# Softmax maxima spread over the partitions: transposes on TensorE, or a round trip through HBM and a ScalarE copy into PSUM

## The chip, the core and the metric

The kernel runs on one core of a Trainium2 chip (trn2). Time is device microseconds of one execution; 3 runs of the kernel before are given. TensorE is PE (its weight loads are PEld), VectorE is DVE, ScalarE is ACT, GpSimd is POOL, and SyncE is SP, which issues nearly all DMAs from one queue, in order.

## What is computed

Everything is float32. Eight images of 512 channels and 32x32 positions go through two layers. The first is a group norm, then a block of 1x1 and 3x3 convolutions with two attention stages, then a residual sum. The second is a group norm, a masked 1x1 convolution and a residual sum. The change touches the attention:

```python
def bot_attention(x, qkv_w, rw, rh):
    b, c, h, w = x.shape
    hw = h * w                                        # 1024 positions
    qkv = conv2d(x, qkv_w, 0).reshape(b, 3, HEADS, HD, hw)   # 4 heads of 64
    q, k, v = (qkv[:, 0], qkv[:, 1], qkv[:, 2])
    r = (rw + rh).reshape(1, HEADS, HD, hw)
    logits = jnp.einsum('bhdi,bhdj->bhij', q, k + r) * HD ** (-0.5)
    a = jax.nn.softmax(logits, axis=-1)
    out = jnp.einsum('bhij,bhdj->bhdi', a, v)
    return out.reshape(b, c, h, w)
```

## The kernel before

**Units.** Attention is cut into 64 units (`class Unit`): image `n`, block `i` of two, head pair `hp`, and `half` of the 1024 queries. A unit's name is `n_i_hp_half`, so `2_1_1_1` is the last unit of image 2 in block 1. Logits lie transposed, keys on the partitions and 512 queries along the free dimension, two heads side by side. A unit has eight key tiles `t` (KT = 8) of 128 keys.

**The steps of a unit.** `logits(t)` multiplies (L494, tile `lg`, a PSUM bank for each head), copies both banks into the SBUF tile `st` (ScalarE, L500), and takes a running maximum over the key tiles into `mx` (VectorE, L505). `mx` then holds, for each query, a maximum for each of the 128 partitions. `top()` transposes `mx` in blocks of 128 queries on TensorE (L513, PSUM tile `mt`), so that queries lie on partitions, and reduces along the free dimension with a change of sign (VectorE, L514). The result is the small tile `nm`, 128x2x4, with the negated maximum of every query. The softmax needs that number on all 128 partitions, again along the free dimension. `spread()` does this: eight transposes, each of a column of `nm` stretched to 128x128 by a step of zero (L521), into the two-bank PSUM tile `mb`. `soften(t)` adds `mb` to `st` (VectorE, L525) and exponentiates in place (ScalarE, L526); GpSimd sums the exponentials of all tiles (L531). `values(t)` multiplies `st` by `v` into `po` (TensorE, L537). `finish()` sums over partitions with a matrix of ones (L549, `den`), copies it (L551), and `divide()` takes the reciprocal on VectorE (L556) and scales `po`.

**Who sets the order.** The main loop (L980 to L1036) goes through 16 slots of an image and a block, four units each. It writes out the steps of a unit, the logits of the next unit between them, and other work of the same or other images as filler: `advance(share)` takes pieces from `slot_filler` (3x3 convolutions of the next slot, projections, and the 1x1 convolutions of the `Background` list) until a share of the slot's filler is done. A slot has 4 x 10 such steps. `Clock` holds operations that are due some time later by an estimate of passed time. The framework's scheduler then orders each engine's instructions by its own estimate of when each could start; `in_turn` and `add_manual_dep` with `IN_ORDER` fix the order of some without a wait. Each engine executes its own queue strictly in that order, so an instruction that waits holds up all behind it.

**Memory.** PSUM's eight banks are `ps_m` (2 banks, `mb`), `ps_o` (1 bank, `po`) and `ps_f` (5 banks in rotation, for all else). In SBUF, `st` tiles come from 10 buffers, the weights from 4, `k` and `v` from 3 each, and the temporaries of the 3x3 convolution's input transform (`wt`: `a`, `b`, `a2`, `b2`) from 3. The small parameters (`bn_sb`, `s_sb`, `rw_sb`, `rh_sb`, and `tri`) have tiles of their own. The helper `load` (L77) issues a DMA on SP.

The step before the first exponentials in the main loop is this:

```python
u.top()
clock.tick(0.9)
advance((base + 1) / steps)
u.spread()
clock.tick(0.9)
advance((base + 2) / steps)
```

Of the kernel before, what the change touches and what calls it, by code (L numbers as in the profile page):

```python
# [15 lines left out]
F32 = mybir.dt.float32  # L16
# [6 lines left out]
P = 128  # L23
# [16 lines left out]
def conv_preact_kernel(ctx: ExitStack, tc: tile.TileContext, x, cv1, cv2, mcv1, qkv, mcv2, bn, rw, rh, conv, s_in, t_in, out):  # L40
# [18 lines left out]
    tp = pool("tp", 3)  # L59
    wt = pool("wt", 3)  # L60
    ps_m = pool("ps_m", 1, space=PSUM)
# [23 lines left out]

    bn_sb = const.tile([P, 4, BN_ALL], F32, name="bn_sb")
    s_sb = const.tile([P, 2, CT, NG], F32, name="s_sb")
    rw_sb = const.tile([P, NBLK, IT, F], F32, name="rw_sb")
    rh_sb = const.tile([P, NBLK, IT, F], F32, name="rh_sb")

# [4 lines left out]

    y_dram = [[dram.tile([P, IT, HW], F32, name=f"y_{n}_{j}") for j in range(4)] for n in range(NB)]
    x2_dram = [dram.tile([P, 2, CT, HALF], F32, name=f"x2_{n}") for n in range(NB)]

# [70 lines left out]


    def accumulate(ps, terms):


        for n, (w, moving) in enumerate(terms):
            nc.tensor.matmul(ps, w, moving, start=(n == 0), stop=(n == len(terms) - 1))  # L175
            if n % 2 and n < len(terms) - 1:
                yield 1.72
        return Whole(1.72)
# [22 lines left out]
    class Image:  # L201
# [76 lines left out]
        def conv3(self, i):  # L278
# [12 lines left out]
            def product(r, u):  # L291
                w = weights(f"w_m1_{name}_{r}", (IT, IT, 3, P), w_m1[i][r])
                ps = bank(f"m1_{name}_{r}")
                terms = [(c, dx) for c in range(IT) for dx in range(3)]
                for co in range(IT):
                    for j, (c, dx) in enumerate(terms):
                        nc.tensor.matmul(  # L297
                            ps[:, ts(co, 256)].rearrange("p (t x) -> p t x", x=F),
                            w[:, co, c, dx],
                            u[:, 9 * c : 9 * c + 8, dx : dx + F],  # L300
                            start=(j == 0),
                            stop=(j == len(terms) - 1),
                        )
# [174 lines left out]
    class Unit:  # L478
        def __init__(self, im, i, hp, half):
            self.name = f"{im.n}_{i}_{hp}_{half}"  # L480
            self.im, self.hp, self.half = im, hp, half
            self.st, self.mx = [], None

        def begin(self):
# [22 lines left out]
        def top(self):  # L507

            self.nm = small.tile([P, 2, 4], F32, tag="nm", name=f"nm_{self.name}")
            for h in range(2):  # L510
# [3 lines left out]
                nc.vector.tensor_reduce(self.nm[:, h], mt, AX.X, ALU.max, negate=True)  # L514

        def spread(self):

            self.mb = pair(ps_m, "mb", f"mb_{self.name}")
            for h in range(2):
                for c in range(4):  # L520
                    nc.tensor.transpose(self.mb[:, h, ts(c, P)], self.nm[:, h, c : c + 1].to_broadcast([P, P]), ident)  # L521

# [85 lines left out]
    def last_weights():  # L608
# [48 lines left out]

        tri = small.tile([P, P], F32, tag="tri", bufs=1, name="tri")
        nc.gpsimd.affine_select(
# [321 lines left out]
    for s in range(len(slots)):  # L981
# [22 lines left out]
        for j in range(4):  # L1004
# [91 lines left out]
```

## Time and profile before

| | |
|---|---|
| median of 3 runs | 3276.86 us (3268.33 to 3284.32) |
| the profiled execution | 3278.47 us, span 3276.7 us |
| mean granted TensorE clock | 0.990 |
| PE busy | 3159.1 us (96%) |
| DVE busy | 2045.9 us (62%) |
| ACT busy | 1756.6 us (54%) |
| POOL busy | 1219.1 us (37%) |
| DMA | 399.30 MB, mean 122 GB/s |

A line of a group reads: source line, engine, operation, written tile and read tiles, shape, count, then busy time in us with the mean of one in ns, then the idle time of the engine just ahead of these instructions and what ended most of it. A line of waits reads: who waited, for whom, then total us, how often, and the longest. A timeline line reads: start, duration (both us), engine, source line, operation, tiles, shape, count, and in brackets the idle time before. A line of DMA issues ends with the KB of each and the median us from issue to landing. Float32 matmuls stand as two passes each, so counts are twice the program's; the transposes of L513 and L521 stand once.

### The profile page before, as it was taken

To read this page: it belongs to the slowest core of one execution; us is meant where nothing else is said; L and a number is where in the kernel's file an instruction comes from. 1 tells how busy PE (TensorE), PEld (TensorE's weight loads), DVE (VectorE), ACT (ScalarE), POOL (GpSimd) and SP (SyncE) were. 2 spreads that over 40 slices of the span, in tenths; PEclk is the share of its full clock that TensorE was granted. 3 is DMA by queue.
4 is the path that set the end of the run, shared out by engine and by line. 5 is a ranking of instruction groups with operands and counts; after the bars stand their busy time and mean duration, and the time that the engine had idled before them with its cause. 6 is when DMAs were issued, how large, how long until landed. Compare 5 with 4: busy or idle time off the path is not lost.

```text
span 3276.7 us, 33257 instructions
## 1 busy us (share of the span) xinstructions
PE 3159.1 (96%) x11716; PEld 1538.0 (47%) x11716; DVE 2045.9 (62%) x2717; ACT 1756.6 (54%) x2369; POOL 1219.1 (37%) x971
## 2 busy tenths in 40 slices
PE   7999999998999999999999999999999999999998
PEld 3645345353545445354545445354445444453343
DVE  5436566666666575767666675767656676666642
ACT  3245765854545655644545555644655554646631
POOL 2104433335334343344334343444334433444420
PEclk9999999999999999999999999999999999999999
DMA  8752352330323241423323341423333341423366
GB/s 292 275 171 71 119 170 94 116 106 20 121 98 106 75 148 55 161 84 106 122 98 105 104 144 54 161 84 108 124 105 108 101 141 49 160 71 116 111 217 205
DMA packets 142007, 399.30 MB, mean 122 GB/s; under 512 B 13072, under 2 KB 14352, under 8 KB 141840
## 3 DMA queue, kind: packets, MB, share of 16 engines
q1 hardware_dynamic: 141120, 396.94, 36.1%
q8 instruction: 93, 1.52, 0.2%
q14 instruction: 74, 0.61, 0.1%
q10 hardware_dynamic: 720, 0.23, 0.0%
HBM read 317.42 MB, written 79.69 MB: 121 GB/s over the span
## 4 chain that ended last, share of the span: by engine, by line
PE 69%; DVE 11%; issue 5%; ACT 4%; DMA 4%; POOL 1%; POOLq 0%; SPq 0%; ACTq 0%; DVEq 0%
PE cv L175 14%; PE m L297 12%; PE po L537 11%; PE lg L494 10%; PE qk L175 6%; PE l L175 5%; PE v L389 3%; DVE st L525 3%; PE mt L513 2%; PE m L175 2%; DVE rb L556 2%; DVE mx L505 2%; PE den L549 2%; PE mb L521 2%; DMA x<-in_x 1%
## 5 line engine op out<-in xcount | busy, mean ns | idle before, releaser
L531 POOL TENSOR_TENSOR sum<-sum,st 128x512 f32<-128x512 f32 x768 | 973.9, 1299 | 771.5 <-ACT st L526 771.5
L526 ACT ACTIVATE st<-st 128x1024 f32<-128x1024 f32 x512 | 534.3, 1056 | 471.4 <-DVE st L525 464.8
L505 DVE TENSOR_TENSOR mx<-mx,lg 128x512 f32<-128x512 f32 x768 | 479.3, 681 | 434.1 <-ACT st L500 433.6
L500 ACT COPY st<-lg 128x512 f32<-128x512 f32 x1024 | 528.1, 594 | 246.1 <-PE lg L494 189.9
L525 DVE TENSOR_TENSOR st<-st,mb 128x1024 f32<-128x1024 f32 x512 | 604.2, 1213 | 79.8 <-PE mb L521 79.8
L297 PE MATMUL m<-plane,w_m 128*128 128x256 f32 x2304 | 534.0, 386 | 18.0 <-DVE z L351 8.3
L494 PE MATMUL lg<-q,k 64*128 64x512 f32 x2048 | 534.6, 618 | 10.4 <-ACT rb L551 3.3
L537 PE MATMUL po<-st,v 128*64 128x512 f32 x2048 | 509.5, 609 | 17.2 <-ACT st L526 11.4
L297 PEld LDWEIGHTS m<-plane,w_m 128*128 128x128 f32 x2304 | 431.4, 191 | 142.7 <-issue 40.8
L531 POOL TENSOR_TENSOR sum<-st,st 128x512 f32<-128x512 f32 x128 | 162.2, 1288 | 834.1 <-ACT st L526 712.0
L175 PE MATMUL cv<-y,w_cv 128*128 128x512 f32 x1024 | 466.5, 600 | 4.9 <-DVE mx L505 2.1
L494 PEld LDWEIGHTS lg<-q,k 64*128 64x128 f32 x2048 | 188.9, 186 | 346.2 <-issue 236.5
L175 PEld LDWEIGHTS cv<-y,w_cv 128*128 128x128 f32 x1024 | 185.5, 190 | 252.0 <-issue 231.6
L537 PEld LDWEIGHTS po<-st,v 128*64 128x64 f32 x2048 | 125.2, 136 | 327.6 <-issue 231.6
L556 DVE RECIPROCAL rb<-rb 128x256 f32<-128x256 f32 x128 | 216.1, 1725 | 66.0 <-ACT rb L551 66.0
L175 PE MATMUL cv<-x,w_cv 128*128 128x512 f32 x512 | 242.2, 622 | 12.3 <-DVE mx L505 4.1
L175 PE MATMUL l<-x,w_l 128*128 128x512 f32 x512 | 235.2, 604 | 9.6 <-DVE mx L505 6.2
L175 PE MATMUL qk<-z,w_qkv 128*128 128x512 f32 x512 | 234.2, 600 | 1.6 <-DVE mx L505 1.6
L514 DVE TENSOR_REDUCE nm<-mt 128x4 f32<-128x512 f32 x128 | 83.0, 685 | 221.5 <-PE mt L513 221.2
L130 ACT ACT_TABLE_LOAD x122 | 156.5, 1283 | 14.7 <-PE m L175 6.4
L175 PEld LDWEIGHTS cv<-x,w_cv 128*128 128x128 f32 x512 | 97.0, 197 | 138.7 <-issue 112.1
L175 PEld LDWEIGHTS l<-x,w_l 128*128 128x128 f32 x512 | 93.3, 191 | 133.6 <-issue 106.5
(144 smaller groups left out, 2342.1 us busy)
## 6 DMA issues: line engine op xcount, KB each, us to landing
w_m<-w_m SPq DMA_DIRECT2D x96, 768.0 KB, 4.4
w_cv<-in_cv SPq DMA_DIRECT2D x90, 512.0 KB, 3.5
y<-y SPq DMA_DIRECT2D x64, 512.0 KB, 4.7
x<-in_x SPq DMA_DIRECT2D x56, 512.0 KB, 5.2
y<-y SPq DMA_DIRECT2D x64, 256.0 KB, 3.6
k<-r SPq DMA_DIRECT2D x32, 512.0 KB, 3.8
res<-y SPq DMA_DIRECT2D x32, 512.0 KB, 4.2
xr<-in_x SPq DMA_DIRECT2D x32, 512.0 KB, 4.3
```

The lines of the kernel that those rows point to most:

```text
L130: nc.scalar.activation(dst, src, AF.Silu, bias=bn_b[:, col : col + 1], scale=bn_s[:, col : col + 1])
L175: nc.tensor.matmul(ps, w, moving, start=(n == 0), stop=(n == len(terms) - 1))
L297: nc.tensor.matmul(ps[:, ts(co, 256)].rearrange("p (t x) -> p t x", x=F), w[:, co, c, dx], u[:, 9 * c : 9 * c + 8, dx : dx + F], start=(j ...
L389: nc.tensor.matmul(ps[:, ts(j, P)], z[:, c, ts(4 * j4 + j, P)], w[:, c, 512 + P * hp : 512 + P * hp + P], start=(c == 0), stop=(c == IT - 1),)
L494: nc.tensor.matmul(lg[h], self.k[r, ts(t, P)], self.q[r, self.hp, ts(self.half, HALF)], start=True, stop=True)
L500: nc.scalar.copy(st[:, h], lg[h])
L505: in_turn(nc.vector.tensor_tensor(self.mx[:, h], so_far[:, h], lg[h], ALU.max))
L525: in_turn(nc.vector.tensor_tensor(st, st, flat(self.mb), ALU.add))
L526: nc.scalar.activation(st, st, AF.Exp)
L531: nc.gpsimd.tensor_tensor(self.acc[:, h], so_far[:, h], self.st[t][:, h], ALU.add)
L537: nc.tensor.matmul(self.po[HD * h : HD * h + HD], self.v[:, t, ts(h, HD)], self.st[t][:, h], start=(t == 0), stop=(t == KT - 1),)
L556: nc.vector.reciprocal(self.rb[:, r], self.rb[:, r])
```

## The change

The negated maxima reach all partitions by another way. `top()` now ends with two DMAs on SP. The first writes `nm` to a small tensor in HBM (`nm_dram`, one for each unit), reordered so that the 1024 numbers lie in the order of the queries. The second reads these 4 KB into all 128 partitions of a new SBUF tile `wide`. `spread()` is one ScalarE copy of `wide` into `mb`. The rest of a unit reads `mb` as before. In the main loop `spread()` and the first two `soften` steps stand later: behind the filler up to step 2.5, `finish()` of the unit before, and the next unit's first two key tiles of logits. `latest` remembers the last matmul written; the copy is ordered after it, without a wait. `wide` takes 4 KB of each partition. For it, `wt` has two buffers in place of three, and the small parameters share one `k` buffer (`par`) at the start.

```diff
-    wt = pool("wt", 3)
+    wt = pool("wt", 2)
...
-    bn_sb = const.tile([P, 4, BN_ALL], F32, name="bn_sb")
-    s_sb = const.tile([P, 2, CT, NG], F32, name="s_sb")
-    rw_sb = const.tile([P, NBLK, IT, F], F32, name="rw_sb")
-    rh_sb = const.tile([P, NBLK, IT, F], F32, name="rh_sb")
+    par = kp_.tile([P, HW], F32, tag="k", name="par")
...
+    nm_dram = [dram.tile([2, 4, P], F32, name=f"nm_{n}") for n in range(64)]
...
-            nc.tensor.matmul(ps, w, moving, start=(n == 0), stop=(n == len(terms) - 1))
+            latest[:] = [nc.tensor.matmul(ps, w, moving, start=(n == 0), stop=(n == len(terms) - 1))]
...
                 nc.vector.tensor_reduce(self.nm[:, h], mt, AX.X, ALU.max, negate=True)
 
+            d = nm_dram[self.number]
+            with nc.allow_non_contiguous_dma(reason="1024 numbers"):
+                load(d.rearrange("h c p -> p h c"), self.nm)
+            self.wide = one.tile([P, 2 * HALF], F32, tag="wide", name=f"wide_{self.name}")
+            load(self.wide, d.rearrange("h c p -> (h c p)").partition_broadcast(P))
+
         def spread(self):
 
             self.mb = pair(ps_m, "mb", f"mb_{self.name}")
-            for h in range(2):
-                for c in range(4):
-                    nc.tensor.transpose(self.mb[:, h, ts(c, P)], self.nm[:, h, c : c + 1].to_broadcast([P, P]), ident)
+            copy = nc.scalar.copy(flat(self.mb), self.wide)
+            tc.add_manual_dep(copy.ins, latest[0].ins.name, IN_ORDER, reason="not before it can be there")
...
             u.top()
-            clock.tick(0.9)
-            advance((base + 1) / steps)
-            u.spread()
-            clock.tick(0.9)
+            clock.tick(0.5)
             advance((base + 2) / steps)
             if before:
                 before.finish()
                 clock.tick(0.9)
             for t in range(0, KT, 2):
-                u.soften(t)
-                if before and t == 0:
-                    before.divide(1)
-                u.soften(t + 1)
                 if t:
+                    u.soften(t)
+                    u.soften(t + 1)
                     u.values(t - 2)
                     u.values(t - 1)
                     clock.tick(2.0)
                 if nxt:
                     nxt.logits(t)
                     nxt.logits(t + 1)
                     clock.tick(2.0)
+                if t == 0:
+                    advance((base + 2.5) / steps)
+                    u.spread()
+                    u.soften(0)
+                    if before:
+                        before.divide(1)
+                    u.soften(1)
                 advance((base + 4 + t) / steps)
```

More of the change, by code (lines that the diff above doesn't have):

```diff
@@ L83, in weights, with param @@
         return t
-    bn_sb = const.tile([P, 4, BN_ALL], F32, name="bn_sb")
-    s_sb = const.tile([P, 2, CT, NG], F32, name="s_sb")
-    rw_sb = const.tile([P, NBLK, IT, F], F32, name="rw_sb")
-    rh_sb = const.tile([P, NBLK, IT, F], F32, name="rh_sb")
+    par = kp_.tile([P, HW], F32, tag="k", name="par")
+    def param(first, shape):
+        return par[:, first : first + P].rearrange("p (a b c) -> p a b c", b=shape[0], c=shape[1])
+    s_sb = param(0, (CT, NG))
+    rw_sb = param(128, (IT, F))
+    rh_sb = param(256, (IT, F))
+    bn_sb = par[:, 512 : 512 + 4 * BN_ALL].rearrange("p (a b) -> p a b", b=BN_ALL)
     w_m1 = [[dram.tile([P, IT, IT, 3, P], F32, name=f"w_m1_{i}_{r}") for r in range(6)] for i in range(NBLK)]
@@ L168, in conv_preact_kernel @@
         pass
+    latest = []
     def accumulate(ps, terms):
         for n, (w, moving) in enumerate(terms):
-            nc.tensor.matmul(ps, w, moving, start=(n == 0), stop=(n == len(terms) - 1))
+            latest[:] = [nc.tensor.matmul(ps, w, moving, start=(n == 0), stop=(n == len(terms) - 1))]
             if n % 2 and n < len(terms) - 1:
@@ L296, in product @@
                     for j, (c, dx) in enumerate(terms):
[L297 to L303, printed above, removed]
+                        latest[:] = [
+                            nc.tensor.matmul(
+                                ps[:, ts(co, 256)].rearrange("p (t x) -> p t x", x=F),
+                                w[:, co, c, dx],
+                                u[:, 9 * c : 9 * c + 8, dx : dx + F],
+                                start=(j == 0),
+                                stop=(j == len(terms) - 1),
+                            )
+                        ]
                         if j % 3 == 2 and (co, j) != (1, 5):
@@ L482, in __init__ @@
             self.st, self.mx = [], None
+            self.number = 8 * (2 * im.n + i) // 2 + 2 * hp + half
         def begin(self):
@@ L656, in last_weights @@
         yield
-        tri = small.tile([P, P], F32, tag="tri", bufs=1, name="tri")
+        tri = par[:, 384:512]
         nc.gpsimd.affine_select(
```

## The prediction

> **What bounds the kernel now.** I read the page first: its busy times, then the chain of work that ended last.
>
> ```profile
> PE 3159.1 (96%) x11716; PEld 1538.0 (47%) x11716; DVE 2045.9 (62%) x2717; ACT 1756.6 (54%) x2369; POOL 1219.1 (37%) x971
> PE 69%; DVE 11%; issue 5%; ACT 4%; DMA 4%; POOL 1%; POOLq 0%; SPq 0%; ACTq 0%; DVEq 0%
> ```
>
> TensorE is busy for 96% of the span and idle for 117.6 us in all, so PE work that goes is time that goes, unless something else becomes late. Next the groups by line and shape:
>
> ```profile
> L521 PE MATMUL mb<-ident,nm 128*128 128x128 f32 x512 | 67.9, 276 | 0.0
> L525 DVE TENSOR_TENSOR st<-st,mb 128x1024 f32<-128x1024 f32 x512 | 604.2, 1213 | 79.8 <-PE mb L521 79.8
> L526 ACT ACTIVATE st<-st 128x1024 f32<-128x1024 f32 x512 | 534.3, 1056 | 471.4 <-DVE st L525 464.8
> L514 DVE TENSOR_REDUCE nm<-mt 128x4 f32<-128x512 f32 x128 | 83.0, 685 | 221.5 <-PE mt L513 221.2
> ```
>
> The 512 transposes of `spread` (eight in each of 64 units) hold PE for 67.9 us, 2.1% of the span. VectorE waits 79.8 us for them. Who pays for that shows in PE's own waits:
>
> ```profile
> PE gm_a L146 <- DVE mv_a L144: 19.8, 3, 14.2
> PE po L537 <- ACT st L526: 11.4, 6, 4.4
> PE m L297 <- DMA w_m<-w_m: 2.8, 2, 1.8
> ```
>
> PE waits only 11.4 us for exponentials and 2.8 us for weights. The timeline of the tightest kind of unit (`2_1_1_1`) shows the path:
>
> ```profile
> 1492.93 1.09 PE L513 MATMUL mt<-ident,mx 128*128 128x128 f32 x8
> 1493.63 1.29 DVE L514 TENSOR_REDUCE nm<-mt 128x4 f32<-128x512 f32 x2 [5.63 <-PE mt L513]
> 1494.96 1.09 PE L521 MATMUL mb<-ident,nm 128*128 128x128 f32 x8
> 1496.15 1.22 DVE L525 TENSOR_TENSOR st<-st,mb 128x1024 f32<-128x1024 f32 x1 [1.24 <-PE mb L521]
> 1498.67 1.06 ACT L526 ACTIVATE st<-st 128x1024 f32<-128x1024 f32 x1
> 1501.86 1.08 PE L537 MATMUL po<-st,v 128*64 128x512 f32 x4
> ```
>
> From the end of the maxima's transposes (1494.02) the negated maxima are there after 0.90 us, the broadcast after 2.03 us, the first exponential after 5.71 us, and PE asks for it at 7.84 us. Over the 64 units the timeline gives a mean of 6.9 us for the exponential against 14.1 us until PE asks. That lead is what the change spends.
>
> **The change, part by part.** *Removed:* 67.9 us of PE work, all of it in a stream that PE fills. The 11.4 us of waits at `po` go too, since I count the waits there anew.
>
> *Added path.* The new path goes from the negated maxima through a store, a load and a ScalarE copy to the first add. The store writes 1024 separate 4-byte elements, 64 on each of 16 DMA engines. The load reads the same 4 KB for 128 partitions, 512 KB in all. Their nearest rows:
>
> ```profile
> y<-res SPq DMA_DIRECT2D x32, 256.0 KB, 2.6
> k<-r SPq DMA_DIRECT2D x32, 512.0 KB, 3.8
> ybuf<-y SPq DMA_DIRECT2D x16, 512.0 KB, 7.5
> ```
>
> Store: the trace's packet records have 4-byte packets (the semaphore writes, 12608 of them) at a median of 9 ns, and 2 KB packets at 84 ns. 64 of the first take 0.58 us, about what the 8 packets per engine of a 256 KB store take (0.67), so I take that store's 2.6 us. Its fastest landing is 2.3, the low end; at 84 ns for every element it would be 2.3 - 0.67 + 5.4 = 7.0, the high end. Load: `k<-r` has the same shape, 3.8 (fastest 3.1); the slowest row of that size, two loads at once, is 7.5. With 0.9 for the reductions and 0.1 per hand-over the broadcast has landed at L = 0.9 + 0.1 + 2.6 + 0.1 + 3.8 = 7.5 us after the transposes (6.5 to 15.6).
>
> The copy of 128x1024 into PSUM has no row: between one 1024-wide ACTIVATE (1.06) and two 512-wide copies (1.19), I take 1.05. After it come the add (1.21), the exponential (1.06) and 0.2 of hand-overs, so the exponential is there at L + 3.5 = 11.0.
>
> *Cover.* I summed, from the instruction orders of both programs, the PE work between the last maxima transpose and the first `po` of each unit, at what one matmul costs in the groups (a matmul is two passes in the trace: lg 0.52, m1 0.46, l 0.92, den 0.61). For the kernel before this gives 14.2 us, and the trace shows 14.1, so the sum can be trusted. For the changed order it is 14.4 on average: the scheduler moves the same work into the gap. But it is uneven. 49 units have 13.5 to 17.8; `3_0_0_1` has 26 m1, 2 den and 4 lg = 15.4. Fifteen are short, most of them `_1_1_1` units with little filler: one of 5.9, six of 8.1 (`2_1_1_1`: 2 den, 8 lg, 3 l), four of 9.1, three of 10.6, one of 11.3.
>
> *Long units.* ScalarE's order puts the copy behind the next unit's first four `lg` copies, so it gets there at +8 to +11 whatever the transfers do. `3_0_0_1`: copy from 9.4, exponential at 12.8, PE asks at 15.4. Nothing is lost, and 2 us are spare; without that cover each further us would cost 49 us.
>
> *Short units.* Shortage is 11.0 minus cover: 5.1 + 6 x 2.9 + 4 x 1.9 + 3 x 0.4 = 31 us. Later exponentials of the same units stand behind Silu work and table loads (1.28 each) on ScalarE; going through ScalarE's order for all eight of every unit adds 12, so 43 us. The same count gives 30 at L = 6.5, 66 at 9, 81 at 10, 128 at 12, 234 at 14.
>
> *SP's queue.* Each load waits for its store, so SP stands 2.6 us per unit. In the trace the issues that precede each store in the new order had gone out by +1.7 us (one at +5.1), so stores leave at once. Between store and load there is often a weight load, or a `res` load issued at +4 to +5, which makes L two us later in three of the 9.1 units: 6 us. Behind the load wait weight and image loads, which PE hardly waits for now (2.8 us): I take 5 us, from 0 to 20.
>
> *ScalarE* gains 64 copies (67 us) and loses table loads, 244 to 210 in the order (34 x 1.28 = 44). At 54% busy this is hidden by its idle time; if not, 0.4 us per unit, 23 us. *VectorE's* order now has both reciprocals (3.4), the maxima and a residual add ahead of the first add, so it reaches it at about +8 in the short units: no new bound at L = 7.5, since the copy ends at 8.6. GpSimd's sums start some 6 us later in units of 50, with 18 us of work each. Two `wt` buffers for three and the parameters in a `k` buffer cost nothing: the temporaries are made and read in VectorE's own order, and the third `k` buffer is asked for after the last parameter is read. Were they not hidden, 16 transforms would wait one 0.9 us operation each.
>
> *Sum:* span 3276.7 - 67.9 - 11.4 + 43 + 6 + 5 = 3251.4; with the 1.8 us that lie around the span (3278.5 profiled) 3253, and the median of the runs is 1.6 lower: **3252**.
>
> **Two rules of the skill against these rows.** In the row no load of the trace reads the same bytes for all partitions, so 3.8 us is taken from loads that spread over HBM. The Trainium skill, "DMA: Bandwidth & Descriptors", section "Latency and other measured facts", reports that copies whose partitions hit the same HBM channels in step fell from 207 to 103 GB/s. It calls the mechanism an inference, and no run here shows it yet. If the broadcast fell to 103 GB/s, an estimate from that page is 5.1 us for the bytes, some 2.5 more: L = 10, and the gain would be gone.
>
> The second concerns the store, where the 9 ns packets above say the elements are cheap. The same page, "Rules for kernel authors", says that a non-contiguous last dimension becomes one descriptor per element and should be rearranged. It gives no price per element; by its fit of 2.0 us plus bytes over 436 GB/s (for another way of issuing) the store would take 2.0, the load 3.2, L would be 6.3, and the time about 15 us lower than mine.
>
> **Rivals.** *A, the forecast (0.50):* the gain is eaten by half in the short units. L from 6.5 to 8.5 gives 3276.9 - 79.3 + (30 to 58) + (0 to 11), 3228 to 3267.
>
> *B, slower (0.26):* the two transfers together need over 9 us, and the wait moves to `po`. It decides at L = 10, where shortage equals the gain. At L = 12 it is 3276.9 - 79.3 + 128 + 11 = 3337, at 14 it is 3443. For it speaks that neither transfer's form is in the trace and that landings are seen up to 7.5 us; against it the 9 ns packets and DMA engines 32% busy between 230 and 3000 us.
>
> *C, no change (0.24):* only 69% of the chain lies on PE, so about 0.69 x 68 = 47 us of the removed work was on the path, and the short units give back 43: 3273. For it speaks the chain's passage through VectorE at 1497 to 1520 us, just where units are short; against it that PE's own idle time is so small.
>
> **How the numbers follow.** A measurement can tell about 0.5%, 16 us, from no change, so faster means under 3260. A holds 0.50, C 0.24, B 0.26. The range goes from A's low end to B at L = 12: 3228 to 3335.
>
> **What would show it.** Right: no `mb` group on PE, `po` waiting 40 to 60 us for ScalarE, nearly all in the fifteen units; store near 2.6, load near 3.8, copy near 1.1 us; VectorE's 79.8 us of waiting now on ScalarE and larger. Wrong: a load over 6 us, `po` waits in most of the 64 units, or PE waiting for weights behind SP.

## The result, and the profile after

The change makes the kernel slower: 3857.99 us (median of 6 runs, 3846.76 to 3867.03) against 3277.19 us (6 runs, 3268.33 to 3284.32). The ratio is 1.1768, with a 95% interval of 1.1746 to 1.179. The forecast was 3252 us, with a range that ended at 3335.

The page of the changed kernel, its busy line, the slices of TensorE and its granted clock, and the groups that answer to L521, L525, L526, L514 and L537 of before:

```profile
PE 3338.2 (86%) x11204; PEld 1539.0 (40%) x11204; DVE 2042.1 (53%) x2717; ACT 1787.5 (46%) x2399; POOL 1215.6 (31%) x971
PE   7988888887988988888889888887888888887898
PEclk9999899988988998898989998998998998898899
```
```profile
L555 PE MATMUL po<-st,v 128*64 128x512 f32 x2048 | 607.9, 696 | 292.1 <-ACT st L544 278.5 <-DVE q L576 13.4
L543 DVE TENSOR_TENSOR st<-st,mb 128x1024 f32<-128x1024 f32 x512 | 604.2, 1214 | 325.5 <-ACT mb L538 325.5
L544 ACT ACTIVATE st<-st 128x1024 f32<-128x1024 f32 x512 | 533.6, 1056 | 302.1 <-DVE st L543 293.5 <-DVE gms_b L155 0.8
L526 DVE TENSOR_REDUCE nm<-mt 128x4 f32<-128x512 f32 x128 | 83.1, 685 | 217.7 <-PE mt L525 217.7
L538 ACT COPY mb<-wide 128x1024 f32<-128x1024 f32 x64 | 65.0, 1016 | 523.0 <-DMA wide<-nm 523.0
```

TensorE has 512 transposes fewer and yet is busy 179 us longer and idle 526 us in place of 118 us: 408 + 179 = 587, the whole growth of the span (3864.1 against 3276.7). Most of the idle time comes with a unit's first `po`: 440 of the 526 us lie between the last transpose of a unit's maxima and that matmul (25 in the kernel before), and 278.5 us stand directly ahead of `po`. The waits of TensorE and SyncE (who for whom, total, times, longest) and the median landings say why:

```profile
PE po L555 <- ACT st L544: 278.5, 57, 12.0
PE lg L506 <- DVE mx L517: 29.0, 11, 7.9
```
```profile
SPq L78 <- DMA nm<-nm: 531.1, 60, 10.6
```
```profile
wide<-nm SPq DMA_DIRECT2D x64, 512.0 KB, 5.3
k<-r SPq DMA_DIRECT2D x32, 512.0 KB, 3.6
nm<-nm SPq DMA_DIRECT2D x64, 4.0 KB, 10.3
```

The store of 4 KB takes 10.3 us, four times the forecast. The timeline of the unit that was shown before, `2_1_1_1`, shows the chain (start, duration, engine, operation, idle time before):

```profile
1722.80 1.09 PE L525 MATMUL mt<-ident,mx 128*128 128x128 f32 x8
1723.49 1.29 DVE L526 TENSOR_REDUCE nm<-mt 128x4 f32<-128x512 f32 x2 [5.63 <-PE mt L525]
1724.81 0.37 SPq L78 DMA_DIRECT2D nm<-nm  x1
...
1734.19 0.32 SPq L78 DMA_DIRECT2D wide<-nm  x1
...
1739.94 1.02 ACT L538 COPY mb<-wide 128x1024 f32<-128x1024 f32 x1 [11.85 <-DMA wide<-nm]
1741.06 2.35 DVE L543 TENSOR_TENSOR st<-st,mb 128x1024 f32<-128x1024 f32 x2 [9.71 <-ACT mb L538]
1742.32 2.19 ACT L544 ACTIVATE st<-st 128x1024 f32<-128x1024 f32 x2 [1.36 <-DVE st L543]
...
1743.43 1.12 PE L555 MATMUL po<-st,v 128*64 128x512 f32 x2 [10.77 <-ACT st L544]
```

From the end of the transposes (1723.89) the load is issued at 10.3 us, the copy starts at 16.1, the first exponential is there at 19.5, and TensorE has stood idle for 10.8 us. Over the 64 units the means are: store landed 11.4, load landed 16.7, first exponential 21.0, and 6.9 us of idle TensorE in each unit. The other 179 us are fewer instructions that take longer: one `po` pass takes 696 ns in the mean where it took 609 (line of the kernel before below), and the granted clock is 0.916 in place of 0.990. The trace's clock records hold only full and half speed: half for 650 us, against 68 in the kernel before, and 384 of the 2048 `po` passes take over 900 ns (593 is the median before), against 12.

```profile
L537 PE MATMUL po<-st,v 128*64 128x512 f32 x2048 | 509.5, 609 | 17.2 <-ACT st L526 11.4 <-DVE q L558 5.8
```

### The profile page after: what moved, and what is told of

It is laid out like the page before. It is cut to its first block, busy times and chain, and to the rows that moved or that the text cites. A ratio compares the mean times of both kernels' runs of the same rounds, so it can differ in the third digit from the quotient of the medians.

```text
span 3864.1 us, 32498 instructions
## 1 busy us (share of the span) xinstructions
PE 3338.2 (86%) x11204; PEld 1539.0 (40%) x11204; DVE 2042.1 (53%) x2717; ACT 1787.5 (46%) x2399; POOL 1215.6 (31%) x971
## 5 line engine op out<-in xcount | busy, mean ns | idle before, releaser
L555 PE MATMUL po<-st,v 128*64 128x512 f32 x2048 | 607.9, 696 | 292.1 <-ACT st L544 278.5
L506 PE MATMUL lg<-q,k 64*128 64x512 f32 x2048 | 617.0, 650 | 75.8 <-DVE mx L517 29.0
L307 PE MATMUL m<-plane,w_m 128*128 128x256 f32 x2304 | 562.7, 399 | 18.5 <-DVE mx L517 13.5
L307 PEld LDWEIGHTS m<-plane,w_m 128*128 128x128 f32 x2304 | 444.0, 198 | 179.9 <-issue 58.5
L184 PE MATMUL cv<-y,w_cv 128*128 128x512 f32 x1024 | 480.9, 619 | 24.6 <-DMA y<-y 20.9
L506 PEld LDWEIGHTS lg<-q,k 64*128 64x128 f32 x2048 | 210.8, 195 | 473.1 <-issue 292.4
L555 PEld LDWEIGHTS po<-st,v 128*64 128x64 f32 x2048 | 137.6, 150 | 656.9 <-ACT st L544 383.5
L538 ACT COPY mb<-wide 128x1024 f32<-128x1024 f32 x64 | 65.0, 1016 | 523.0 <-DMA wide<-nm 523.0
L184 PE MATMUL qk<-z,w_qkv 128*128 128x512 f32 x512 | 247.1, 628 | 33.0 <-ACT rb L569 22.3
L526 DVE TENSOR_REDUCE nm<-mt 128x4 f32<-128x512 f32 x128 | 83.1, 685 | 217.7 <-PE mt L525 217.7
L184 PEld LDWEIGHTS qk<-z,w_qkv 128*128 128x128 f32 x512 | 98.5, 201 | 171.9 <-issue 114.7
```

Source lines behind the costliest of these rows:

```text
L184: latest[:] = [nc.tensor.matmul(ps, w, moving, start=(n == 0), stop=(n == len(terms) - 1))]
L307: nc.tensor.matmul(ps[:, ts(co, 256)].rearrange("p (t x) -> p t x", x=F), w[:, co, c, dx], u[:, 9 * c : 9 * c + 8, dx : dx + F], start=(j ...
L506: nc.tensor.matmul(lg[h], self.k[r, ts(t, P)], self.q[r, self.hp, ts(self.half, HALF)], start=True, stop=True)
L538: copy = nc.scalar.copy(flat(self.mb), self.wide)
L555: nc.tensor.matmul(self.po[HD * h : HD * h + HD], self.v[:, t, ts(h, HD)], self.st[t][:, h], start=(t == 0), stop=(t == KT - 1),)
```

## The experiments

Times are medians; each run stood beside runs of the kernel before on the same chip, whose medians lie between 3275 and 3279 us. "Lead" is the time from the end of an exponential to the first `po` matmul that reads it, a mean over the 64 units, worked out from the trace.

**1. The store as rows.** A partition's eight numbers go out as one row of 32 bytes:

```diff
-                load(d.rearrange("h c p -> p h c"), self.nm)
+                load(d.rearrange("h c p -> (h c p)").rearrange("(p h c) -> p h c", h=2, c=4), self.nm)
```

> The store of the 1024 negated maxima goes out as 128 rows of 32 bytes instead of 1024 separate elements of 4 bytes: same bytes, same queue, same place in the order, same broadcast load and copy behind it. (The numbers reach the wrong queries in this kernel; it is run for its time only.) In the changed kernel this store landed 10.2 us after its issue, though all of its 4-byte packets had been processed within 1.6 us. Theory, the separate elements are what lands late: the store lands 2.3 to 3.5 us after issue, the broadcast is there 9 to 10 us after the maxima's transposes instead of 16.7, TensorE's idle time up to the first po falls from 440 to below 120 us, the granted clock is back at 0.98 or more, and the time is 3260 to 3330 us. Rival, any write to HBM that is read back at once costs this much, whatever its shape: the store still takes 8 to 10 us and the time stays above 3750. Rival, the moved order alone costs the time: the store is fast and the time stays above 3600.

Measured: 3346.53 us, ratio 1.0187 (1.0152 to 1.0221), clock 0.984. The store lands after 1.4 us, the load after 4.5 (4.7 for `w_m` in the same table), and the broadcast is there at 7.9 us, near the 7.5 of the forecast's sum.

```profile
w_m<-w_m SPq DMA_DIRECT2D x96, 768.0 KB, 4.7
wide<-nm SPq DMA_DIRECT2D x64, 512.0 KB, 4.5
nm<-nm SPq DMA_DIRECT2D x64, 4.0 KB, 1.4
```

The separate elements cost 511 us. But the time ends 17 us above what was expected, and 68 us above the kernel before. Something else is wrong too.

**2. Later exponentials.** `advance((base + 2.5) / steps)` ahead of `spread` becomes `(base + 6)`. In this kernel some filler work then comes ahead of the second half of the preceding unit's division, whose result it reads; only the time is used.

> All of the change kept, but spread (copy and first exponentials) is written later: filler work up to (base + 6) / steps is taken before it instead of (base + 2.5) / steps. In the built order the TensorE work between the last transposes of the maxima and the first po rises from a mean of 14.4 to 21.1 us (lower quartile 19.1; a few units still at 6 to 12), and the sum of what is short of an exponential at 20 us falls from 361 to 101 us. Theory, the late exponential is the whole cause (idle time first, and the lower clock because of the idle time): store and load stay at 10 and 5 us, idle time up to the first po falls from 440 to 100-160 us, the granted clock rises to 0.97 or more, and the time is 3270 to 3400 us. Rival, the 4-byte packets or the DMA load slow the core in itself (clock, contention): the idle time falls but the time stays above 3500.

Measured: 3597.45 us, clock 0.953: the theory's number is missed by 200 us, and the rival's (above 3500 with less idle time) is met; experiment 4 takes that rival up. Store and load stay at 10.0 and 5.7 us, but the copy now stands behind later work on ScalarE, the first exponential comes at 23.3 us and not at 20, just when TensorE asks (23.6). The idle time up to `po` falls from 440 to 203 us. More cover helps, but it drags the exponentials along.

**3. The moved order with TensorE's transposes.** Store, load and copy are replaced by the eight transposes.

```diff
...
-            copy = nc.scalar.copy(flat(self.mb), self.wide)
-            tc.add_manual_dep(copy.ins, latest[0].ins.name, IN_ORDER, reason="not before it can be there")
+            for h in range(2):
+                for c in range(4):
+                    nc.tensor.transpose(self.mb[:, h, ts(c, P)], self.nm[:, h, c : c + 1].to_broadcast([P, P]), ident)
```

> The change's moved order, its two wt buffers and its parameters in a k buffer are kept, but spread is done by the eight TensorE transposes of the kernel before, without store, load and copy. Theory, only the round trip through HBM is late: within 20 us of the kernel before (3255 to 3300 us), granted clock 0.98 or more. Rival, the moved order (first exponentials behind the next unit's first logits and the filler work) costs the time by itself: 3400 us or more, with TensorE waiting for exponentials in most units.

Measured: 3349.0 us, ratio 1.0214 (1.0198 to 1.0229), clock 0.987. Neither theory had this size. With no transfer at all the moved order is 70 us slower, as much as the kernel with rows.

**4. A 4-byte store that nobody waits for.** The kernel of experiment 1, and behind the broadcast load:

```diff
+    nm_side = [dram.tile([2, 4, P], F32, name=f"nms_{n}") for n in range(64)]
...
+            with nc.allow_non_contiguous_dma(reason="1024 numbers"):
+                load(nm_side[self.number].rearrange("h c p -> p h c"), self.nm)
```

> The kernel with 128 rows of 32 bytes, and beside it, issued right after the broadcast load, the store of 1024 separate 4-byte elements to a second tensor in HBM that nobody reads or waits for. (As there, the numbers reach the wrong queries.) Theory, the 4-byte store costs only by its own late landing, which here nothing waits for: within 30 us of the kernel with 128 rows. Rival, 64 stores of 1024 elements hold up the DMA engines or HBM for the other transfers: 100 us or more above it, with weight and image loads landing 2 us or more later.

Measured: 3747.86 us, ratio 1.1432 (1.1407 to 1.1457). The rival is right, and my theory of a cost by its own landing alone falls.

```profile
wide<-nm SPq DMA_DIRECT2D x64, 512.0 KB, 10.9
nm<-nm SPq DMA_DIRECT2D x64, 4.0 KB, 1.4
nms<-nm SPq DMA_DIRECT2D x64, 4.0 KB, 10.7
```

The load that is issued just before the 4-byte store lands with it, after 10.9 us instead of 4.5. Weight loads land only 1.1 us later (`w_m` 5.8 against 4.7), less than the rival said; it is the broadcast, on which the exponentials wait, that lands 6.4 us later. The packet records show the engines standing: counted from the side store's issue, 38 packets of 4 KB start in the two us from +2 (mean of a unit), then 3 to 6 in each us from +4 to +10, then 22 and 43 in the next two. The 4-byte packets themselves are recorded at 7 to 9 ns, and nearly all of them have started by +3. So the store holds up the load that is in flight beside it, and its own packet records don't show it.

**5. The moved order alone.** The kernel before with nothing but the new loop (the last hunk of the diff).

> The kernel before with one part of the change: the loop that writes the order (spread and the first two exponentials behind the next unit's first logits and the filler work up to (base + 2.5) / steps). Transposes, three wt buffers and separate parameter tiles as before. Theory, the order itself costs the 70 us that the kernel with the moved order and PE transposes showed: 3330 to 3365 us, with PE waiting 30 us or more at po. Rival, the two wt buffers or the parameters in a k buffer cost it: 3265 to 3295 us.

Measured: 3341.26 us, ratio 1.0198 (1.0173 to 1.0222), clock 0.990. The theory holds: the order costs 62 us. Two `wt` buffers and `par`, which experiment 3 has and this one doesn't, make at most the 8 us between the two.

```profile
PE po L537 <- ACT st L526: 41.7, 52, 3.0
PE m L297 <- DVE mx L505: 20.2, 12, 3.4
```

**6. The form of the store.** Behind the rows a second store of one of eight forms, to the same tensor, ahead of the load (`form = (self.number + self.number // 8) % 8`; for forms 0 to 3 `e = 1 << form`, and `load(row.rearrange("(g p e) -> p g e", p=P, e=e), nm.rearrange("p (g e) -> p g e", e=e))`).

> The kernel with 128 rows of 32 bytes, and after that store, to the same tensor and ahead of the broadcast load, a second store whose form goes round with the unit, eight units for each of eight forms: 1024, 512, 256 and 128 elements of 4, 8, 16 and 32 bytes (4 KB in all), 128, 256 and 512 elements of 4 bytes, and 1024 elements of 32 bytes (from the maxima, to a tensor that nobody reads). (As before, the numbers reach other queries than their own.) Only the landing of the second store is looked at. Theory, each separate element costs the same time whatever its size: from 1.4 us for 128 and 10.2 for 1024 about 10 ns each, so 128 elements land at 1.4 us, 256 at 2.6, 512 at 5 and 1024 at 10, with 4 or 32 bytes alike. Rival, what costs is the few bytes: 1024 elements of 32 bytes land in 4 us or less, and 512 of 8 bytes well before 512 of 4. Rival, it is the scattered addresses in SBUF or HBM as such, with a step: all 4-byte forms at 8 us or more.

**7. The step of the store.** The same, with the step between elements in HBM as the variable.

> As with the eight forms: the kernel with 128 rows of 32 bytes and behind that store, to the same tensor, a second one whose form goes round with the unit; only its landing is looked at. (The numbers reach other queries than their own.) 128 elements of 4 bytes with a step in HBM of 4, 32, 64 and 512 bytes; 1024 of 4 bytes with a step of 64; 128 of 8 bytes with steps of 8 and 64; 128 of 32 bytes with a step of 512. Theory, writes to the same line of HBM wait for one another: 128 elements of 4 bytes side by side land at 8.2 us again, with a step of 64 or 512 at 1.4 to 2.5, 1024 with a step of 64 at 2.4 to 4; 128 of 8 bytes side by side at 4 to 5 and with a step of 64 at 1.4 to 2.5. Rival, a small element costs by its size, wherever it goes: every 4-byte form at 8 us or more, 8 bytes at 4 to 5 with either step.

Measured in both, issue to landing of the second store, eight of each:

| elements x bytes | step in HBM | least us | median us |
|---|---|---|---|
| 1024 x 4 | 4 | 8.62 | 11.02 |
| 512 x 4 | 4 | 8.26 | 9.48 |
| 256 x 4 | 4 | 7.76 | 8.48 |
| 128 x 4 | 4 | 6.92 | 8.17 |
| 128 x 4 (again) | 4 | 6.93 | 8.06 |
| 128 x 4 | 32 | 1.38 | 3.02 |
| 128 x 4 | 64 | 1.39 | 2.17 |
| 128 x 4 | 512 | 1.39 | 3.10 |
| 1024 x 4 | 64 | 2.49 | 3.56 |
| 512 x 8 | 8 | 3.72 | 5.03 |
| 128 x 8 | 8 | 2.80 | 4.42 |
| 128 x 8 | 64 | 1.39 | 3.19 |
| 256 x 16 | 16 | 1.56 | 3.28 |
| 128 x 32 | 512 | 1.40 | 2.91 |
| 1024 x 32 (from `mx`) | 32 | 2.14 | 2.43 |

My theory of experiment 6, a price for each element, falls: 128 elements of 4 bytes take 8 us and 1024 of 32 bytes 2.4. Nor is it the size: 4 bytes with a step of 32 land at 1.4. It is neighbours in HBM: with eight writes to the same 32 bytes a store takes 6.9 to 8.6 us at least, with four 2.8 to 3.7, with two 1.6, with one 1.4. Experiment 7's theory holds, and a step of 32 bytes is already enough, not only one of 64. Whether writes collide within 32 bytes or within 16 stays open. The 16-byte neighbours land 0.16 us after the 32-byte rows at the least (1.56 against 1.40), and their greater number alone may cost that: by an estimate from 1024 and 128 elements of 4 bytes with a step of 64 (2.49 against 1.39), 128 more elements cost 0.16.

**8. A busier TensorE.** Twelve matmuls of no use behind each unit's transposes, in the changed kernel:

```diff
+            self.mb = pair(ps_m, "mb", f"mb_{self.name}")
+            for n in range(12):
+                nc.tensor.matmul(self.mb[:, n % 2], ident, self.mx[:, n % 2], start=True, stop=True)
...
-            self.mb = pair(ps_m, "mb", f"mb_{self.name}")
```

> The changed kernel with more work on TensorE: behind the maxima's transposes of each unit 12 matmuls of 128x512 are added (into the PSUM banks that the ScalarE copy then overwrites; their result is not used), 768 in all, about 0.55 us each or 6.6 us for each unit and 420 us in all. They fill about the 6.9 us that TensorE stands idle before po in each unit. Theory, the clock fell because TensorE stood idle: the idle time up to po falls from 440 to below 150 us, the granted clock rises from 0.916 to 0.97 or more, and the time FALLS though work is added, to 3640 to 3790 us. Rival, the clock fell for another reason (DMA, or the core's load as a whole): the clock stays below 0.94, and the time is 3850 us or more.

Measured: 4042.62 us; idle time up to `po` 72 us. The expected fall did not come, since one added matmul took 0.88 us, not 0.55, and overfilled the gap. The clock is the answer here:

```profile
core 0: 4044.9 us, clock 0.981
```

**9. Six of them.**

> As with the 12 added matmuls for each unit, but 6: the added matmul took 0.88 us there, so this adds 5.3 us to each unit, 338 us in all, and does not overfill the 6.9 us that TensorE stood idle before po. Theory, idle TensorE is what lowers its clock: clock 0.955 or more where the changed kernel has 0.916, idle time up to po from 440 to 100-200 us, and 3720 to 3830 us, less than the changed kernel's 3858 though it has 338 us more work. Rival, the added work costs what it fills, and the clock is another matter: 3860 us or more.

Measured: 3876.02 us, clock 0.958, idle time up to `po` 199 us. Clock and idle time are as the theory said, but the time did not fall and meets the rival's 3860 or more. Yet the 344 us that the added matmuls keep TensorE busy cost 18 us. Without them its busy time is 3580 - 344 = 3236 us, 102 less than in the changed kernel for the same instructions. So the lower clock follows the idle time, and what it costs was overrated. The Trainium skill, "TensorE: Matmul & The Clock Gate", Part 1, says that the clock halves after an idle window of about 3.4 us. The clock records of the changed kernel agree in part: 65 of the 66 gaps of TensorE over 3.4 us end in half clock or have it within 3.4 us behind them, but so do 22 of the 32 gaps between 1 and 3.4 us.

**10. Without the copy.** The kernel with rows, and VectorE adds from `wide` itself (`in_turn(nc.vector.tensor_tensor(st, st, self.wide, ALU.add))`).

> The kernel with 128 rows of 32 bytes, without the ScalarE copy into PSUM: VectorE's add reads the broadcast from the SBUF tile that the load fills. (The numbers reach other queries than their own.) Theory, the copy and what it queues behind on ScalarE are on the way to the first exponential: the first add starts 1 to 2.5 us earlier after the transposes than 11.9, the po waits fall from 55 to below 35 us, and the time is 3295 to 3335 us, against 3347 with the copy. Rival, VectorE's own queue (reciprocals, the next unit's maxima) holds the add there: the add starts within 0.5 us of 11.9 and the time within 10 us of 3347. Rival, an add with both operands in SBUF is slower than the 1.21 us with one in PSUM: VectorE's busy time grows, and the time is above 3360.

Measured: 3399.65 us, 53 us slower than with the copy: the second rival.

```profile
L541 DVE TENSOR_TENSOR st<-st,wide 128x1024 f32<-128x1024 f32 x512 | 731.4, 1459 | 11.7 <-DMA wide<-nm 11.7
```

With both operands in SBUF the add takes 1459 ns in place of 1213, and GpSimd's sums slow down beside it (its busy time 1357 us in place of 1217).

**11. Numbers at hand.** The changed kernel without store and load; the copy reads a tile of zeros. Then the same with the loop of the kernel before.

```diff
+    given = one.tile([P, 2 * HALF], F32, tag="wide", name="given")
+    nc.vector.memset(given, 0.0)
...
+            self.wide = given
```

> The changed kernel without store and load: the ScalarE copy into PSUM reads a tile of zeros that is filled once at the start, so nothing is subtracted before the exponential. Transposes and reductions of the maxima still run, the broadcast's transposes are gone, the moved order is kept. Theory, the removed transposes are a gain of 60 to 79 us and the round trip of 8 us takes it back: 3265 to 3295 us, some 62 us above what the order of the kernel before would give. Rival, the transposes were no gain under this order, since the exponentials set the pace: 3330 us or more, as with 128 rows of 32 bytes (3346).

> As the kernel with the tile of zeros (nothing subtracted before the exponential, no store, no load), with the loop of the kernel before: spread behind filler work up to (base + 1) / steps, first exponentials ahead of the next unit's logits. This is the removed term by itself. Theory of the prediction's sum, TensorE's 68 us go from the time whole, with up to 11 us of waits: 3195 to 3220 us. Rival C of the prediction, only the 69% of the chain that lies on TensorE counts: 3225 to 3240. Rival, no gain: 3260 or more.

Measured: 3340.38 us with the moved order, 3213.82 us with the order of before (ratio 0.9802, 0.9788 to 0.9817). TensorE's busy lines, moved order first:

```profile
PE 3168.3 (95%) x11204; PEld 1489.7 (45%) x11204; DVE 2043.1 (61%) x2718; ACT 1782.3 (54%) x2401; POOL 1216.9 (37%) x971
```
```profile
PE 3091.4 (96%) x11204; PEld 1478.2 (46%) x11204; DVE 2038.2 (63%) x2718; ACT 1825.6 (57%) x2441; POOL 1222.5 (38%) x971
```

With the order of before the removed transposes are worth 64.5 us. The busy time falls from 3159.1 to 3091.4, by just their 67.9. With the moved order nothing is left of it, though no number is late: the second rival of the first expectation. TensorE's weight loads for `po` then wait for exponentials at 162 places, against 42 with the order of before (36.9 us):

```profile
PEld po L553 <- ACT st L542: 166.1, 162, 3.9
```

**12. Earlier start.** With the order of before, the transposes, store and load of a unit are issued during the preceding unit, and its last logits stand ahead of that unit's values of tiles 4 and 5. First with rows and a copy that reads in steps of 32 bytes to put the numbers in order; then with 256 elements of 16 bytes and a straight copy.

```diff
...
+                if nxt and t == KT - 2:
+                    advance((base + 8.5) / steps)
+                    nxt.top()
                 advance((base + 4 + t) / steps)
```

> A version meant to keep what the change removes. Store in 128 rows of 32 bytes, the ScalarE copy puts the numbers back in order as it reads (steps of 32 bytes within a partition), spread and the first exponentials where the kernel before has them, and the maxima's transposes, store and load of a unit are issued earlier: during the preceding unit, behind its values of tiles 4 and 5 and filler work up to (base + 8.5) / steps, and ahead of its last values. In the built order the TensorE work from the last transposes to the first po is then 17.9 us on average (lower quartile 16.2, least 8.2), where the kernel before has 14.2. Theory, the 68 us of transposes are a gain once the round trip is both short (broadcast landed 8 us after the transposes, first exponential at 11.5 to 12.5) and started early: waits at po of 20 to 60 us, granted clock 0.985 or more, 3215 to 3265 us. Rival, TensorE waits at the transposes instead, since the maxima come less long behind their logits there (2.5 us of TensorE work at least, 4.4 in the middle, against 7.6 before): waits at mt of 60 us or more and 3280 us or more.

> The version with the early start, with the numbers put in order otherwise: the maxima's transposes take every fourth query, so that a partition's four numbers of a head are neighbours, the store has 256 elements of 16 bytes, and the ScalarE copy reads the broadcast straight (about 1.04 us instead of 2.01). Theory, the long copy in ScalarE's and VectorE's queues cost the early version most of its loss against the kernel with 128 rows (3380 against 3346): 3300 to 3345 us. Rival, the earlier transposes and the crowded end of a unit cost it: 3360 us or more.

Measured: 3380.33 and 3368.71 us. The theory falls in both. The copy in steps took 2014 ns, and without it the time is only 12 us less. Nor does the rival's wait of 60 us at `mt` show (22 to 23 us in both). In the second kernel the first exponential comes 13.7 us after the transposes with a lead of 4.9 us, TensorE waits 39 us at `po`, and the clock is 0.978. What makes up the rest of the loss stays open.

**13. The round trip in the order of before.** 256 elements of 16 bytes, copy and first exponentials ahead of the next unit's logits; copy behind or ahead of the division:

```diff
...
             u.top()
             clock.tick(0.5)
             advance((base + 2) / steps)
             if before:
                 before.finish()
                 clock.tick(0.9)
+            u.spread()
             for t in range(0, KT, 2):
+                u.soften(t)
...
```

> The change's removal of the transposes with the order of the kernel before: 256 elements of 16 bytes (the maxima's transposes take every fourth query, so that the numbers arrive in order), the broadcast load, the copy of 1.04 us, and copy and first two exponentials ahead of the next unit's first logits; only the copy stands one place later than the kernel before has its transposes, behind the division of the preceding unit (base + 2). With zeros ready at once the same order took 3214 us; here the first exponential comes at 11 to 13 us instead of 5.8, ahead of po at 13.7 in the long units and 2 to 5 us late in the fifteen short ones. Theory, the moved order was the second mistake, and 8 us fit in front of po: 3214 plus 15 times 2 to 4 us, 3230 to 3275. Rival, VectorE and ScalarE stand still for the broadcast and the next unit's logits and maxima come late for it: 3300 us or more.

> As that kernel, with the copy at the very place where the kernel before has its transposes (base + 1), ahead of the copy of the preceding unit's denominators on ScalarE, which then waits for the broadcast. Theory, the waiting copy delays the division by up to 4 us and frees po late: 5 to 30 us above the kernel with the copy behind the division. Rival, ScalarE has room enough there: within 5 us of it.

Measured: 3384.93 and 3387.96 us. The place makes no difference, and the round trip costs 171 us against numbers at hand: the first expectation's rival by its number. Its wait shows as well: VectorE stands 110 us for the copy, against 42 with zeros at hand. The rest of the way to 171 us is not taken apart.

**14. Transfers that nobody waits for.** The order of before, a copy of ones that are at hand, and store and load beside it, once in rows and once with 4-byte elements; one is added to each number in the place of the subtraction.

```diff
...
+            load(one.tile([P, 2 * HALF], F32, tag="aside", name=f"aside_{self.name}"), d.rearrange("h c p -> (h c p)").partition_broadcast(P))
+            self.wide = ones.unsqueeze(1).to_broadcast([P, 8, P])
```

> The order of the kernel before, a ScalarE copy of ones that are at hand (one is added to each number before the exponential, in the place of the maxima's subtraction), and beside it store (128 rows of 32 bytes) and broadcast load as in the kernel with rows, into a tile that nobody reads. Theory, the late numbers are all of the 171 us: within 15 us of 3214. Rival, the store that SyncE waits for, and the traffic, cost by themselves: 3250 us or more, with weight loads landing later and TensorE waiting for them.

> The same with the change's store of 1024 4-byte elements; again nobody waits for store or load but SyncE's queue, which stands about 10 us for each store. (One is added to each number in the place of the maxima's subtraction.) Theory, most of the 4-byte store's cost is the late numbers: 3214 to 3290 us here. Rival, it is what the store does to weight and image loads, which wait behind it in SyncE's queue and on the DMA engines: 3350 us or more, with TensorE and VectorE waiting for DMA.

Measured: 3215.11 and 3285.93 us. The theory holds in both. Traffic and SyncE's waiting are free with rows (1 us); with 4-byte elements they cost 71 us. TensorE then waits for late divisions (21.6 us, 13.6 with rows) and for `y`, a convolution's input that comes from HBM:

```profile
PE po L555 <- DVE q L576: 21.6, 16, 8.0
PE cv L184 <- DMA y<-y: 20.2, 6, 5.3
```

What the runs have in common is the first exponential. Means of the 64 units, from the end of the transposes of the maxima:

| kernel | first exponential us | its lead us | time us |
|---|---|---|---|
| before | 6.9 | 7.2 | 3277 |
| order of before, zeros at hand | 5.8 | 7.2 | 3214 |
| the same, 4-byte store aside | 5.8 | 8.0 | 3286 |
| order of before, round trip with 16-byte elements | 13.0 | 1.4 | 3385 |
| moved order, zeros at hand | 13.9 | 0.6 | 3340 |
| moved order, TensorE's transposes (loop alone) | 14.2 | 0.5 | 3341 |
| moved order, rows | 14.4 | 0.6 | 3347 |
| changed kernel, later exponentials | 23.3 | 0.3 | 3597 |
| changed kernel | 21.0 | 0.7 | 3858 |

Under the moved order the first exponential comes at 14 us whether the numbers are at hand, on TensorE or 8 us away, because it is written behind the next unit's first logits, on ScalarE and VectorE too. `po` then takes it with half a microsecond to spare in the mean, and less than 0.8 us in 46 to 49 of the 64 units.

No version with the maxima subtracted beat the kernel before. The two that are faster leave them out.

## Why the prediction was wrong, step by step

The sum of the runs, each step a difference of two kernels:

| step | from the runs | forecast |
|---|---|---|
| 512 transposes and their waits go (zeros at hand) | -64.5 | -79.3 |
| moved order | +127 | 0 |
| round trip of 8 us in that order (rows) | +6 | +54 (43 + 6 + 5) |
| 4-byte elements in place of rows | +511 | 0 |

They sum to 580, the measured difference is 581. The split goes by this order of steps: with TensorE's transposes still there the moved order costs 62 us, and taking them out then gains 1 us (3341.26 to 3340.38).

**The removed work was sized rightly, for the order of before.** The 67.9 us went whole there, so rival C, which counted 69% of it, is out. The 11.4 us of waits at `po` did not go with them (11.0 with zeros at hand).

**The store failed**: "I take that store's 2.6 us" from 4-byte packets at 9 ns. It landed at 10.3, above even the high end of 7.0. The 4-byte packets of the trace were semaphore writes; these were neighbours in HBM, and the packet's recorded duration does not hold what their writing costs. The rule that spoke against the change was in the text (the Trainium skill, "DMA: Bandwidth & Descriptors", "Rules for kernel authors": a non-contiguous last dimension becomes one descriptor per element), and I let the 9 ns overrule it. The same page, "Specifications", says that below 512 bytes a DMA reads, modifies and writes. These runs draw the line elsewhere: 32-byte rows land at 1.4 us and so do single 4-byte elements with a step of 32.

**The load** was mis-sized mildly: 3.8 forecast, 4.5 with a fast store, 5.3 in the changed kernel. Against `k<-r` (3.6 there) the same bytes for all partitions cost 0.9 us with a fast store, not the 2.5 of the estimate from the skill. With rows L is 7.9, so the sum for L was sound but for the store. (The copy's 1.05 us lies below both rows that it is said to lie between, 1.06 and 1.19; it measured 1.02, so nothing hung on it.)

**Long units failed**: "Nothing is lost, and 2 us are spare". The 49 long units were costed at nothing because the first exponential would still be in time. But the loop alone, with no transfer, takes 62 us, and the removed transposes are eaten on top of it. I counted only whether the first `po` waits, by mean durations, and not the lead, which shrinks from 7.2 us to 0.5: it is under 0.8 us in 49 of the 64 units, where its least had been 2.0.

That this lead had covered small delays is shown in part. From the start of the matmul before to the first `po` pass on a tile's exponential it takes 280 us with the moved loop, summed over all tiles, and 242 before: 38 of the 58 us by which the two profiled spans differ. With zeros at hand it is 39 of 117. Of these 117, 40 are idle time (159 against 119) and 77 longer busy time of TensorE, some 14 of them by half clock (half of the difference of its busy time there, 74 against 46 us). The rest isn't placed. Nor is the lead all: in the second kernel of experiment 12 it is 4.9 us, and the time is 155 us above zeros at hand.

**Idle time was sized about right once L is known, the clock not at all.** The forecast's count gave 234 us of shortage at L = 14, and 361 for an exponential at 20 us (L = 16.5, from the expectation of experiment 2); with L = 16.7 the idle time grew by 408. But a TensorE with longer gaps also runs slower: it is busy for 3338 us here, and for 3183 with rows (clock 0.984) and the same instructions. No term stood for these 155 us. The clock records account for them: TensorE was busy at half clock for 430 us here and 98 with rows, and half of the difference, 166 us, is an estimate of what that adds. Rival B had the mechanism and, with L bounded by the wrong store, ended at 3443.

**SP's queue** (11 us) came to 1 us for a fast store, and to 71 for this one, both under the order of before.

## What to carry to other kernels

Before a small store goes into a loop, look at who shares its 32 bytes of HBM before you count its elements or bytes: put a partition's numbers side by side first, and the same 4 KB land in 1.4 us instead of 10. And when a change spends the lead of a step on the way to the busiest engine, don't ask only whether the step is still in time by mean durations: price the lead itself by moving the order alone, with everything else as it was, as experiment 5 does in one run.

## What the runs showed of the hardware

- 4-byte writes to neighbours in HBM land at 8.2 us for 128 of them and 11.0 for 1024, and hold up other transfers that are in flight (a load 10.9 us in place of 4.5). Their packets are recorded at 7 to 9 ns. With a step of 32 bytes the price is gone (1.4 us at the least).
- The granted clock follows TensorE's gaps: 0.990 with 118 us of idle time, 0.916 with 526, 0.958 and 0.981 when useless work fills part of the gaps. The records hold only full and half speed; gaps over 3.4 us ended in half speed or had it within 3.4 us behind them 65 times in 66, gaps of 1 to 3.4 us 22 times in 32 (changed kernel). 344 us of useless work cost 18 us.
- VectorE's add of 128x1024 float32 takes 1213 ns with one operand in PSUM and 1459 with both in SBUF, with GpSimd's sums running beside it. A ScalarE copy of 128x1024 takes 1.02 to 1.04 us straight and 2.01 us when it reads with a step of 32 bytes.
